# The first thirty products of a 392-product matmul stream: another order of loads, transposes and sums

## The chip, the cores and the metric

The kernel runs on one core of one Trainium2 chip. The metric is the time on the device in microseconds (us), the median of several executions. A core has five engines that run side by side, each through its own instructions in order: TensorE (PE, with weight loads listed apart as PEld), VectorE (DVE), ScalarE (ACT), GpSimd (POOL) and SyncE (SP), which here only issues DMAs. They wait for each other through semaphores.

## The reference

```python
x = L0_attn_data                       # (2, 1024, 512): 2048 rows of 512, float32
xn = _layernorm(x, axis=-1)            # (x - mean) / sqrt(var + 1e-5)
s = einsum('bsk,nk->bsn', xn, weight * block_mask)          # 512 x 512, mask by 32 x 32 blocks
nx = xn * rsqrt(mean(xn * xn) + 1e-5) * ln_w
h = silu(einsum('bsh,ih->bsi', nx, gate_w)) * einsum('bsh,ih->bsi', nx, up_w)   # 1792 columns
g = silu(einsum('bsi,hi->bsh', h, down_w))
x = x + s * g
```

## The kernel before

**Products.** All of it is float32. The wide products (gate and up together, and the masked linear) are done in two nested levels of Strassen's scheme in Winograd's form, which forms seven products in place of eight and pays for it with sums and differences. The rows of x are four tiles of 512 rows (t = 0 to 3); each tile is transposed on TensorE into four chunks of 128 features (c = 0 to 3), so that features lie on partitions. A product is a 128x128 weight times a 128x512 operand, two TensorE instructions of 0.43 us, 0.86 us in all. Seven products make one *instance* (function `instance`); there are 56 instances for the 7 gate and up groups and the masked linear, and a later stage of 7 more sets for the down projection. This text writes j:m for product m (1 to 7) of instance j. Only the start of this stream is changed: instances 0 to 3, which use tiles 0 and 1 alone.

**An instance.** Products 1, 6, 7 and 4 add up one after the other in one PSUM bank (call it x), 5 and 3 in a second (y), and 2 is added to the value that x had after product 1, in a third (z). Between two products of one bank the value has to be read out: the *snapshot* after 5 and after 6, the *total* after 2, 3, 7 and 4. Instances with an even number copy on ACT where nothing is to be added (`prior is None`), and those with an odd number add the even one's result on DVE. The value of x after product 1 gets into z by `seed`: an ACT copy into z's bank, to which product 2 is then added ("seeded", line 338); in instance 0 it goes into a buffer in SBUF instead and is added at the total.

**Operands.** `normalise` (L146 on DVE, L148 on ACT) applies the layer norm in place, from `stats` (L126, L127) and `factors` (L137 to L141, with a square root on ACT between two pieces on DVE). `transpose` (L155) writes a chunk into a PSUM bank, `evacuate` (L163) copies it to SBUF on ACT. `inner_b` forms the operands of products 5, 6, 7 and 4 as differences (all `add` calls have line L97); q 1 stands for instance 0 (chunks 0 and 1), q 2 for instance 1 (chunks 2 and 3). For 5, 6 and 7 one input comes straight from the bank of a transposed chunk of tile 1. So the bank of a chunk of tile 1 has two kinds of readers, ACT's copy and DVE's differences. `scale_a` multiplies the first weights by ln_w, `inner_a` forms sums of them on POOL.

**Banks.** PSUM has eight: three with tag X, two Y, one Z, two V (line 91). Transposed chunks share the tags of the products. A bank is handed on when all that read it are through.

**Order.** Nothing is scheduled by a planner. Every operation is put on a list with a position, `at(position, function)`, the list is sorted by position, and each engine runs its own operations in that order. A position is counted in products: 7j plus an offset for instance j. `T(us)` turns a wanted time into a position. `EARLY` gives single products another position than their instance would. `warm` has TensorE multiply the identity by itself until the first tile is there. Loads are issued at the very start, in the order in which they are called, nearly all by SP; each x tile is four loads of 256 KB, each first-level weight block is one of 256 KB.

The seven products of an instance, with offset, bank, snapshot and total, are this table:

```python
            (0, 1, "X", True, None, None),
            (2, 5, "Y", True, ("s5", 3), None),
            (3, 2, "Z", True, None, (None, 0)),
            (4, 6, "X", False, ("s2", 1), None),
            (6, 3, "Y", False, None, ("s2", 1)),
            (8, 7, "X", False, None, ("s5", 3)),
            (12, 4, "X", False, None, (None, 2)),
```

Of the kernel before, what the change touches and what calls it, by code (L numbers as in the profile page):

```python
# [14 lines left out]
P = 128  # L15
# [16 lines left out]
def tile_masked_linear_gated_ffn(  # L32
# [11 lines left out]
    nc = tc.nc  # L44
    NT, H = x.shape
    KC = H // P
    G = gu.shape[0]
    NTT = NT // W
    TT = W // P
# [16 lines left out]
    EARLY = {}  # L66

    def at(pos, fn, *args):
        events.append((pos, len(events), fn, args))
# [23 lines left out]
    def bank(tag, name):  # L93
        return ps.tile([P, W], F32, tag=tag, name=name, bufs=PSB[tag])

    def add(eng, o, a, b, op=ALU.add):
        eng.tensor_tensor(o, a, b, op)  # L97

    dve, pool, act = nc.vector, nc.gpsimd, nc.scalar


    lnw_sb = const.tile([P, KC], F32, tag="lnw", name="lnw_sb")
# [12 lines left out]
    agg = small.tile([P, NTT, TT, 2], F32, tag="agg", name="agg", bufs=1)  # L115
    rms = small.tile([P, NTT, TT], F32, tag="rms", name="rms", bufs=1)

    def load_x(t):
        for i in range(TT):
            xt[t, i] = mem[:, first_slot[("B6", "vc", "v5", "B4")[t]] + i, :]  # L120
            eng = nc.scalar if t == 0 and i >= 2 else nc.sync
            eng.dma_start(xt[t, i], x[(t * TT + i) * P : (t * TT + i + 1) * P, :])

    def stats(t, i):
        st = small.tile([P, 6], F32, tag="st", name=f"st_{t}_{i}")
# [42 lines left out]
    def rms_factor():  # L168

        def first():  # L170
            nc.vector.tensor_scalar_add(rms, agg[:, :, :, 1], EPS)
            nc.vector.reciprocal(rms, rms)
            nc.vector.tensor_mul(rms, agg[:, :, :, 1], rms)
            nc.vector.tensor_scalar_add(rms, rms, EPS)
        return [first, lambda: nc.scalar.activation(rms, rms, AF.Sqrt)]
# [136 lines left out]
    def inner_a(g, part, k0=0, n=2):  # L312

        if part == 1:
            i, si, qs = F["a1"] + 2 * (g % 3), F["s"] + 2 * (g % 2), (1, 2)
        else:
            i, si, qs = *w_slots(g), BLOCKS
        a, s = slots(i + k0, n), slots(si + k0, n)
        a11, a21, a12, a22 = (a[:, :, k * P : (k + 1) * P] for k in range(4))
        s1, s2, s3, s4 = (s[:, :, k * P : (k + 1) * P] for k in range(4))  # L320
        for k in range(n):
            aop[g, qs[k0 + k]] = {1: a11[:, k], 2: a12[:, k], 3: s4[:, k], 4: a22[:, k],
                                  5: s1[:, k], 6: s2[:, k], 7: s3[:, k]}
        return [lambda: add(pool, s1, a21, a22), lambda: add(pool, s2, s1, a11, ALU.subtract),
                lambda: add(pool, s4, a12, s2, ALU.subtract), lambda: add(pool, s3, a11, a21, ALU.subtract)]
# [7 lines left out]
    def instance(j, g, q, prior, dest, after):  # L333


        st = {}

        seeded = j > 0

        def mm(m, tag, key, first):  # L340
            if first and key not in st:
                st[key] = bank(tag, f"{key}_{j}")
            nc.tensor.matmul(st[key], weights(g, q, m), operand(q, m), start=first and not (key == "z" and seeded),  # L343
                             stop=True, skip_group_check=True)

        def seed():

            if seeded:
                st["z"] = bank("Z", f"z_{j}")
                nc.scalar.copy(st["z"], st["x"])  # L350
            else:
                st["s1"] = slot("s2", f"s1_{j}")
                nc.scalar.copy(st["s1"], st["x"])

        def snap(key, name, i):
            s = st[name] = slot(name, f"{name}_{j}")
            if prior is None:
                nc.scalar.copy(s, st[key])
            else:
                add(dve, s, st[key], prior(i))  # L360

        def total(key, name, i):
            if key == "z" and not seeded:
                name = "s1"
            if name:
                add(dve, dest(i), st[key], st[name])
            elif prior is None:
                nc.scalar.copy(dest(i), st[key])
            else:
                add(dve, dest(i), st[key], prior(i))  # L370

        at(EARLY.get((j, 0), 7 * j + 1), seed)
        for off, m, tag, first, snapshot, out in (
# [8 lines that stand above are left out]
            key, pos = tag.lower(), 7 * j + off  # L382
            at(EARLY.get((j, m), pos), mm, m, tag, key, first)
            if snapshot:
                at(pos + 1, snap, key, *snapshot)
            elif out:

                pos += 2.3 if prior is None and m == 2 and seeded else 1
                at(pos, total, key, *out)
                after(out[1], pos)  # L390

# [261 lines left out]
    where = {gq: j for j, gq in enumerate(order)}  # L653
    N = len(order)
    END = 7 * N
    T = lambda us: (us - 14.9) / 0.86
    EARLY.update({(0, 1): T(11.5), (0, 0): T(12.6), (1, 1): T(12.7), (0, 2): T(12.8)})
    SILU = 26.2
    at(T(-10), load_x, 0)
    at(T(-10), lambda: nc.sync.dma_start(lnw_sb, ln_w))  # L660
    for K in range(2):
        at(T(-10), load_a, 0, K)
    at(T(-10), load_x, 1)
    for K in range(2):
        at(T(-10), load_a, 1, K)
    at(T(-10), load_x, 2)
# [4 lines left out]
    def plan(pos, step, todo):  # L671
        for i, fn in enumerate(todo):
            at(pos + step * i, fn)


    def warm(n, b):
        for _ in range(n):
            nc.tensor.matmul(b[:, :P], ident, ident, start=True, stop=True, skip_group_check=True)

    at(T(1.4), lambda: warm(30, bank("V", "idle")))  # L680
    for t, p, step in ((0, T(8.2), 0), (1, T(13.4), 0), (2, 14.5, 1.3), (3, 22.0, 1.3)):
        plan(p, step, factors(t))
    for i in range(TT):
        half = act if i < 2 else dve
        at(T(4.5 + 0.85 * i), stats, 0, i)
        at(T(9.0 + 0.7 * (i % 2)), normalise, 0, i, half)
        at(T(10.1 + 0.8 * i), stats, 1, i)
        at(T(14.2 + 0.7 * (i % 2)), normalise, 1, i, half)
        for c in range(KC):
            at(T((10.2, 10.6, 11.0, 11.8)[c] + 0.1 * i), transpose, 0, c, (2, 3, 0, 1)[i], "XYYX"[c])  # L690
            at(T(15.3 + 0.4 * c + 0.1 * i), transpose, 1, c, (2, 3, 0, 1)[i], "XVVY"[c])
    at(T(6.0), scale_a, 0, 0, pool)
    at(T(8.2), scale_a, 0, 1, pool)
    for c in range(KC):
        at(T((10.7, 11.3, 11.9, 14.0)[c]), evacuate, 0, c, act)
        at((5.6, T(16.0), 6.0, 3.14)[c], evacuate, 1, c, act)
    for us, q, m in ((15.9, 1, 5), (16.6, 1, 6), (17.2, 1, 7), (17.8, 2, 5), (18.4, 1, 4), (19.0, 2, 6),
                     (19.6, 2, 7), (20.3, 2, 4)):
        at(T(us), inner_b, q, m, dve)
    for q in (1, 2):  # L700
        for k in (0, 1):
            for n in (0, 1):
                at(8, outer_b, q, k, n, None)
    at(T(16.4), scale_a, 1, 0)
    at(5.2, scale_a, 1, 1)
    for i in range(TT):
        at(9.6 + 1.2 * i, stats, 2, i)
        at(17.2 + 1.3 * i, stats, 3, i)
        at((30.2, 37.0, 40.9, 44.0)[i], normalise, 2, i, act)
        at(26.5 + 2.4 * i, normalise, 3, i, dve)  # L710
    plan(22.2, 1.3, rms_factor())

    for t, p0 in ((3, 37.5), (2, 51.5)):
        n = t % 2
# [21 lines left out]
    for g in range(G + 1):  # L736
        p, rest = 7 * where[g, 1], 7 * where[g, BLOCKS[0]]
        for K in range(2):
            if g > 2:
                at(p - 22, load_a, g, K)  # L740
            if g == G:
                at(p - (10.4, 7.3)[K], lambda K=K: mask_a(aq[G, 0, K], 0, K))
            elif g > 1:
                at(p - (10.4, 7.3)[K], scale_a, g, K)
        if g:
            plan(p - 7, 1, inner_a(g, 1))
        else:
            plan(T(7.4), 0, inner_a(0, 1, 0, 1))
            plan(T(10.0), 0, inner_a(0, 1, 1, 1))
        at(rest - 29, load_block, g)  # L750

        def block_sums(g=g):
            for k, fn in enumerate(outer_a(g)):
                todo[g, k] = fn
        at(rest - 20, block_sums)
        if g == G:
            for k, (R, K) in ((1, (1, 0)), (4, (1, 1)), (0, (0, 0)), (3, (0, 1))):
                at(rest - 20.5, lambda k=k, R=R, K=K: mask_a(wblk[G][k], R, K))
        for k, off in enumerate((-19.9, -19.3, -18.1, -17, -15.95, -15.94, -15.93, -15.3, -13.95)):
            at(rest + off, lambda g=g, k=k: todo[g, k]())  # L760
        plan(rest - 13, 2.5, inner_a(g, 2, 0, 5))
# [131 lines left out]
```

## Time and profile before

| | |
|---|---|
| median of 4 runs | 520.54 us (519.5 to 520.89) |
| the profiled execution's own time | 519.5 us |
| its span | 517.7 us |
| TensorE busy | 507.8 us, 98% of the span |
| VectorE, GpSimd, ScalarE busy | 384.8, 342.2, 177.9 us |
| granted TensorE clock | full in every slice |

The span is counted from the first instruction to the last; 1.8 us of the execution's time lie around it. Views used: the timeline (start, duration, engine, line, operation, output and inputs, and in brackets the idle time of the engine before it and what ended it), the list of waits, stretches with the busy time of each engine, and DMA issues with their time to landing. TensorE's 98% include the warming up of the first 10 us. The prediction is about the stretch from 0 to 40 us, in which instances 0 to 3 and most of the preparation lie.

### The profile page before, as it was taken

The numbers are of one execution on the slowest core, as the hardware profiler recorded it, in microseconds if no ns is written. First come the engines' busy times: TensorE is split into PE (matmuls) and PEld (weight loads), VectorE is DVE, ScalarE is ACT, GpSimd is POOL, SyncE is SP. The second block draws the span as 40 slices with busy tenths as digits, with TensorE's granted clock in tenths as the row PEclk, the third lists the DMA queues.
The fourth block names the chain that finished last, engine by engine and source line by source line (L and its number), as shares of the span: only waits on it lengthen the run. The fifth ranks groups of instructions, "written<-read, shape, count | busy, mean of one in ns | idle before, by whom it ended". The sixth has DMA issues, their size and how long they took to land. (4 is left out here: it accounts for less than half of the span.)

```text
span 517.7 us, 4933 instructions
## 1 busy us (share of the span) xinstructions
PE 507.8 (98%) x1277; PEld 231.6 (45%) x1277; DVE 384.8 (74%) x583; ACT 177.9 (34%) x340; POOL 342.2 (66%) x280
## 2 busy tenths in 40 slices
PE   8999999999999999999999999998999999999997
PEld 8444543444444444444444444433444444444444
DVE  5897789876986969789696978979646654467726
ACT  3657644542536344353634434320100101001111
POOL 5422239852695978869597889979553664739960
PEclk9999999999999999999999999999999999999999
DMA  8435466459157574666988466598997599476372
GB/s 299 148 122 203 163 220 220 170 210 342 58 208 227 216 283 182 232 237 211 393 326 287 177 234 239 195 331 313 330 382 270 181 372 331 157 254 210 144 235 82
DMA packets 60460, 121.59 MB, mean 235 GB/s; under 512 B 5760, under 2 KB 13328, under 8 KB 58384
## 3 DMA queue, kind: packets, MB, share of 16 engines
q1 hardware_dynamic: 60144, 120.75, 65.1%
q10 hardware_dynamic: 288, 0.52, 0.3%
q8 instruction: 10, 0.16, 0.1%
q14 instruction: 18, 0.15, 0.1%
HBM read 75.11 MB, written 46.15 MB: 234 GB/s over the span
## 5 line engine op out<-in xcount | busy, mean ns | idle before, releaser
L97 POOL TENSOR_TENSOR mem<-mem 128x512 f32<-128x512 f32 (+4 forms) x243 | 306.3, 1283 | 139.8 <-ACT mem L264 45.6
L343 PE MATMUL x<-mem 128*128 128x512 f32 x448 | 214.3, 595 | 1.8 <-DVE mem L97 1.8
L343 PEld LDWEIGHTS x<-mem 128*128 128x128 f32 x448 | 83.4, 190 | 109.4 <-issue 85.0
L97 DVE TENSOR_TENSOR mem<-x,mem 128x512 f32<-128x512 f32 x136 | 91.8, 684 | 40.9 <-PE x L343 39.3
L343 PE MATMUL y<-mem 128*128 128x512 f32 x224 | 114.6, 593 | 1.6 <-DVE mem L97 1.5
L97 DVE TENSOR_TENSOR mem<-mem 128x512 f32<-128x512 f32 (+2 forms) x64 | 84.4, 1324 | 7.1 <-PE dx L570 4.4
L570 PE MATMUL dx<-mem 128*128 128x512 f32 x174 | 78.3, 592 | 0.0
L97 DVE TENSOR_TENSOR mem<-y,mem 128x512 f32<-128x512 f32 x96 | 65.6, 684 | 10.7 <-PE y L343 8.8
L343 PEld LDWEIGHTS y<-mem 128*128 128x128 f32 x224 | 42.1, 190 | 53.9 <-issue 46.3
L350 ACT COPY z<-x 128x512 f32<-128x512 f32 x55 | 31.5, 573 | 100.2 <-PE x L343 95.6
L343 PE MATMUL z<-mem 128*128 128x512 f32 x112 | 57.3, 593 | 0.5 <-ACT z L350 0.5
L570 PEld LDWEIGHTS dx<-mem 128*128 128x128 f32 x174 | 33.1, 190 | 41.6 <-issue 40.9
L570 PE MATMUL dy<-mem 128*128 128x512 f32 x98 | 44.5, 592 | 0.0
L404 ACT ACTIVATE gate<-mem 128x512 f32<-128x512 f32 x56 | 33.1, 601 | 27.7 <-DVE mem L97 23.3
L409 DVE TENSOR_TENSOR mem<-gate,mem 128x512 f32<-128x512 f32 x56 | 38.0, 681 | 4.5 <-POOL mem L97 3.7
L543 POOL TENSOR_TENSOR mem<-mem 128x512 f32<-128x512 f32 x16 | 25.4, 1596 | 15.8 <-DMA mem<-s_dram 15.6
L343 PEld LDWEIGHTS z<-mem 128*128 128x128 f32 x112 | 21.0, 190 | 26.7 <-issue 24.2
L97 DVE TENSOR_TENSOR mem<-z,mem 128x512 f32<-128x512 f32 x41 | 27.9, 682 | 4.4 <-PE z L343 3.0
L553 ACT ACTIVATE silu<-mem 128x512 f32<-128x512 f32 x15 | 9.0, 602 | 64.6 <-DVE mem L97 48.3
L570 PEld LDWEIGHTS dy<-mem 128*128 128x128 f32 x98 | 18.6, 190 | 23.4 <-issue 23.4
L97 DVE TENSOR_TENSOR mem<-dx,mem 128x512 f32<-128x512 f32 x16 | 11.0, 690 | 20.1 <-PE dx L570 20.1
L570 PE MATMUL dz<-mem 128*128 128x512 f32 x56 | 25.2, 592 | 0.0
(69 smaller groups left out, 280.5 us busy)
## 6 DMA issues: line engine op xcount, KB each, us to landing
h_dram<-mem SPq DMA_DIRECT2D x98, 256.0 KB, 2.1
mem<-h_dram SPq DMA_DIRECT2D x28, 768.0 KB, 6.3
mem<-in_gu SPq DMA_DIRECT2D x42, 256.0 KB, 4.2
acc_dram<-mem SPq DMA_DIRECT2D x8, 1024.0 KB, 3.9
mem<-acc_dram SPq DMA_DIRECT2D x8, 1024.0 KB, 4.8
s_dram<-mem SPq DMA_DIRECT2D x16, 256.0 KB, 2.4
mem<-s_dram SPq DMA_DIRECT2D x16, 256.0 KB, 6.5
mem<-in_x_t SPq DMA_DIRECT2D x16, 256.0 KB, 5.8
```

What stands on the lines that cost most here:

```text
L97: eng.tensor_tensor(o, a, b, op)
L343: nc.tensor.matmul(st[key], weights(g, q, m), operand(q, m), start=first and not (key == "z" and seeded), stop=True, skip_group_check=True)
L350: nc.scalar.copy(st["z"], st["x"])
L404: nc.scalar.activation(gate[key], t(), AF.Silu)
L409: nc.vector.tensor_mul(a(), gate[key], b())
L543: at_later.append(lambda: nc.gpsimd.tensor_tensor(s_tile, s_tile, rms_bc[t], ALU.mult))
L553: nc.scalar.activation(b[0][:, part], y[:, part] if source is None else source(), AF.Silu)
L570: nc.tensor.matmul(st[key], w(), b(), start=first and key != "z", stop=True, skip_group_check=True)
```

## The change

It touches positions and engines of the first 30 or so products and of what feeds them. Tile 0 is loaded by SP alone, its four loads in a row, where two of them were issued by ACT; ln_w's load goes from SP to ACT. The loads of tile 1 and of the first weights alternate. There are 25 warm-up products for 30. Product 1:2 comes fourth, before the transposes of tile 1; for that, instance 1 is no longer seeded: its z is a Y bank of its own, and DVE adds x and instance 0's result into a buffer, which the total adds to z. Two of the eight differences (the operands of 0:4 and 1:4, in the code `inner_b` with q 1 and 2, m 4) and the scaling of the second pair of weights go from DVE and ACT to POOL. Chunk 3 of tile 1 is transposed after the other chunks into a V bank, not a Y bank. Statistics of tile 2 come later by about four positions, and the positions of the rest are shifted.

```diff
@@ -115,11 +115,10 @@
     agg = small.tile([P, NTT, TT, 2], F32, tag="agg", name="agg", bufs=1)
     rms = small.tile([P, NTT, TT], F32, tag="rms", name="rms", bufs=1)
 
-    def load_x(t):
-        for i in range(TT):
+    def load_x(t, part=range(4)):
+        for i in part:
             xt[t, i] = mem[:, first_slot[("B6", "vc", "v5", "B4")[t]] + i, :]
-            eng = nc.scalar if t == 0 and i >= 2 else nc.sync
-            eng.dma_start(xt[t, i], x[(t * TT + i) * P : (t * TT + i + 1) * P, :])
+            nc.sync.dma_start(xt[t, i], x[(t * TT + i) * P : (t * TT + i + 1) * P, :])
 
     def stats(t, i):
         st = small.tile([P, 6], F32, tag="st", name=f"st_{t}_{i}")
@@ -335,11 +334,12 @@
 
         st = {}
 
-        seeded = j > 0
+        seeded = j > 1
+        zbank = "Y" if j == 1 else "Z"
 
         def mm(m, tag, key, first):
             if first and key not in st:
-                st[key] = bank(tag, f"{key}_{j}")
+                st[key] = bank(zbank if key == "z" else tag, f"{key}_{j}")
             nc.tensor.matmul(st[key], weights(g, q, m), operand(q, m), start=first and not (key == "z" and seeded),
                              stop=True, skip_group_check=True)
 
@@ -350,7 +350,10 @@
                 nc.scalar.copy(st["z"], st["x"])
             else:
                 st["s1"] = slot("s2", f"s1_{j}")
-                nc.scalar.copy(st["s1"], st["x"])
+                if prior is None:
+                    nc.scalar.copy(st["s1"], st["x"])
+                else:
+                    add(dve, st["s1"], st["x"], prior(0))
 
         def snap(key, name, i):
             s = st[name] = slot(name, f"{name}_{j}")
@@ -386,6 +389,8 @@
             elif out:
 
                 pos += 2.3 if prior is None and m == 2 and seeded else 1
+                if m == 2:
+                    pos = EARLY.get((j, "z"), pos)
                 at(pos, total, key, *out)
                 after(out[1], pos)
 
@@ -653,14 +658,16 @@
     where = {gq: j for j, gq in enumerate(order)}
     N = len(order)
     END = 7 * N
-    T = lambda us: (us - 14.9) / 0.86
-    EARLY.update({(0, 1): T(11.5), (0, 0): T(12.6), (1, 1): T(12.7), (0, 2): T(12.8)})
+    T = lambda us: (us - 14.4) / 0.86
+    EARLY.update({(0, 1): T(10.4), (1, 1): T(11.3), (0, 2): T(12.2), (1, 2): T(13.1), (0, 0): T(11.95),
+                  (1, 0): 4.5, (0, "z"): T(14.75), (1, "z"): 7.0})
     SILU = 26.2
     at(T(-10), load_x, 0)
-    at(T(-10), lambda: nc.sync.dma_start(lnw_sb, ln_w))
-    for K in range(2):
-        at(T(-10), load_a, 0, K)
-    at(T(-10), load_x, 1)
+    at(T(-10), lambda: nc.scalar.dma_start(lnw_sb, ln_w))
+    for part, K in (((0,), 0), ((1,), 1), ((2, 3), None)):
+        at(T(-10), load_x, 1, part)
+        if K is not None:
+            at(T(-10), load_a, 0, K)
     for K in range(2):
         at(T(-10), load_a, 1, K)
     at(T(-10), load_x, 2)
@@ -677,38 +684,38 @@
         for _ in range(n):
             nc.tensor.matmul(b[:, :P], ident, ident, start=True, stop=True, skip_group_check=True)
 
-    at(T(1.4), lambda: warm(30, bank("V", "idle")))
-    for t, p, step in ((0, T(8.2), 0), (1, T(13.4), 0), (2, 14.5, 1.3), (3, 22.0, 1.3)):
+    at(T(1.4), lambda: warm(25, bank("V", "idle")))
+    for t, p, step in ((0, T(6.9), 0), (1, T(12.55), 0), (2, 20.5, 1.3), (3, 22.6, 1.3)):
         plan(p, step, factors(t))
     for i in range(TT):
         half = act if i < 2 else dve
-        at(T(4.5 + 0.85 * i), stats, 0, i)
-        at(T(9.0 + 0.7 * (i % 2)), normalise, 0, i, half)
-        at(T(10.1 + 0.8 * i), stats, 1, i)
-        at(T(14.2 + 0.7 * (i % 2)), normalise, 1, i, half)
+        at(T(3.4 + 0.85 * i), stats, 0, i)
+        at(T(7.9 + 0.7 * (i % 2)), normalise, 0, i, half)
+        at(T(9.1 + 0.85 * i), stats, 1, i)
+        at(T(13.5 + 0.7 * (i % 2)), normalise, 1, i, half)
         for c in range(KC):
-            at(T((10.2, 10.6, 11.0, 11.8)[c] + 0.1 * i), transpose, 0, c, (2, 3, 0, 1)[i], "XYYX"[c])
-            at(T(15.3 + 0.4 * c + 0.1 * i), transpose, 1, c, (2, 3, 0, 1)[i], "XVVY"[c])
+            at(T((9.1, 9.9, 9.5, 10.3)[c] + 0.1 * i), transpose, 0, c, (2, 3, 0, 1)[i], "XYYX"[c])
+            at(T((14.7, 15.1, 15.5, 16.9)[c] + 0.1 * i), transpose, 1, c, (2, 3, 0, 1)[i], "XVVV"[c])
+    for c in range(KC):
+        at(T((9.7, 10.9, 10.3, 11.5)[c]), evacuate, 0, c, act)
+        at(T((19.2, 15.5, 19.8, 18.6)[c]), evacuate, 1, c, act)
+    for us, q, m, eng in ((15.3, 1, 5, dve), (15.9, 1, 6, dve), (16.6, 1, 7, dve), (17.2, 2, 5, dve), (17.8, 2, 6, dve),
+                          (18.4, 1, 4, pool), (19.9, 2, 7, dve), (19.7, 2, 4, pool)):
+        at(T(us), inner_b, q, m, eng)
     at(T(6.0), scale_a, 0, 0, pool)
-    at(T(8.2), scale_a, 0, 1, pool)
-    for c in range(KC):
-        at(T((10.7, 11.3, 11.9, 14.0)[c]), evacuate, 0, c, act)
-        at((5.6, T(16.0), 6.0, 3.14)[c], evacuate, 1, c, act)
-    for us, q, m in ((15.9, 1, 5), (16.6, 1, 6), (17.2, 1, 7), (17.8, 2, 5), (18.4, 1, 4), (19.0, 2, 6),
-                     (19.6, 2, 7), (20.3, 2, 4)):
-        at(T(us), inner_b, q, m, dve)
+    at(T(6.1), scale_a, 0, 1, pool)
+    for K in range(2):
+        at(T(14.3 + K), scale_a, 1, K, pool)
     for q in (1, 2):
         for k in (0, 1):
             for n in (0, 1):
                 at(8, outer_b, q, k, n, None)
-    at(T(16.4), scale_a, 1, 0)
-    at(5.2, scale_a, 1, 1)
     for i in range(TT):
-        at(9.6 + 1.2 * i, stats, 2, i)
-        at(17.2 + 1.3 * i, stats, 3, i)
+        at(13.5 + 1.2 * i, stats, 2, i)
+        at(18.4 + 1.2 * i, stats, 3, i)
         at((30.2, 37.0, 40.9, 44.0)[i], normalise, 2, i, act)
         at(26.5 + 2.4 * i, normalise, 3, i, dve)
-    plan(22.2, 1.3, rms_factor())
+    plan(23.0, 1.3, rms_factor())
 
     for t, p0 in ((3, 37.5), (2, 51.5)):
         n = t % 2
@@ -745,8 +752,8 @@
         if g:
             plan(p - 7, 1, inner_a(g, 1))
         else:
-            plan(T(7.4), 0, inner_a(0, 1, 0, 1))
-            plan(T(10.0), 0, inner_a(0, 1, 1, 1))
+            plan(T(10.5), 0, inner_a(0, 1, 0, 1))
+            plan(T(12.4), 0, inner_a(0, 1, 1, 1))
         at(rest - 29, load_block, g)
 
         def block_sums(g=g):
```

## The prediction

> **What bounds the kernel now.** I read the page first: TensorE is busy 98% of the span at the full clock, so what a change of the start is worth is how much sooner the stream of products runs without gaps. Then the timeline from 0 to 30 us, for these gaps.
>
> ```profile
> PE 507.8 (98%) x1277; PEld 231.6 (45%) x1277; DVE 384.8 (74%) x583; ACT 177.9 (34%) x340; POOL 342.2 (66%) x280
> ```
>
> ```profile
> 4.39 0.69 DVE L126 BATCH_NORM_STATS2 st<-mem 128x6 f32<-128x512 f32 x1 [4.39 <-DMA mem<-in_x]
> ...
> 8.88 1.52 ACT L148 ACTIVATE mem<-mem,nb,scl 128x512 f32<-128x512 f32 x2 [0.44 <-DVE nb L138]
> ...
> 11.23 1.56 ACT L163 COPY mem<-pt 128x512 f32<-128x512 f32 x3 [0.83 <-PE pt L155]
> ...
> 13.04 0.59 ACT L353 COPY mem<-x 128x512 f32<-128x512 f32 x1 [0.26 <-PE x L343]
> ...
> 14.34 1.52 ACT L148 ACTIVATE mem<-mem,nb,scl 128x512 f32<-128x512 f32 x2
> ...
> 16.71 0.59 ACT L163 COPY mem<-pt 128x512 f32<-128x512 f32 x1 [0.85 <-PE pt L155]
> ...
> 17.33 0.69 DVE L97 TENSOR_TENSOR mem<-pt,mem 128x512 f32<-128x512 f32 x1 [0.36 <-ACT mem L163]
> ...
> 19.97 1.10 PE L343 MATMUL x<-mem 128*128 128x512 f32 x2
> ...
> 21.16 1.10 PE L343 MATMUL y<-mem 128*128 128x512 f32 x2
> ...
> 21.64 0.59 ACT L163 COPY mem<-pt 128x512 f32<-128x512 f32 x1 [0.47 <-DVE mem L97]
> ...
> 22.77 1.12 PE L343 MATMUL z<-mem 128*128 128x512 f32 x2 [0.51 <-ACT z L350]
> ...
> 27.73 1.10 PE L343 MATMUL x<-mem 128*128 128x512 f32 x2 [0.41 <-DVE mem L97]
> ...
> 28.67 1.02 PE L343 MATMUL y<-mem 128*128 128x512 f32 x2
> ```
>
> See three things. 0:7 starts at 19.97, 2:5 at 28.67; between lie eight products of 0.86, 6.88 us, so 1.82 are lost: 1:5 waits for a bank, 1:2 (the z row) for ACT's seed, 1:7 for a snapshot queued on DVE between statistics. Second, two readers of one bank take turns in program order: DVE's difference at 17.33 waits for ACT's copy of that chunk (16.71 to 17.30), ACT's copy at 21.64 for DVE's difference. Third, from the timeline of 30 to 44 us:
>
> ```profile
> 35.40 0.41 DVE L173 TENSOR_TENSOR rms<-agg,rms 128x16 f32<-128x16 f32 x1
> ...
> 35.85 0.65 DVE L174 TENSOR_SCALAR rms<-rms 128x16 f32<-128x16 f32 x1
> ...
> 36.41 0.68 DVE L97 TENSOR_TENSOR mem<-x,mem 128x512 f32<-128x512 f32 x1
> ...
> 37.19 0.69 DVE L97 TENSOR_TENSOR mem<-y,mem 128x512 f32<-128x512 f32 x1
> ...
> 38.11 1.02 PE L343 MATMUL y<-mem 128*128 128x512 f32 x2
> ```
>
> The total of 2:7 (36.41) and the snapshot of 3:5 (37.19 to 37.88) end just before 2:4 (37.25) and 3:3 (38.11) need them. DVE is nearly without a pause from 17.3 to 44: a second bound, right beneath TensorE.
>
> **The change part by part.** *Loads.* Before, the first load shares the engines with ACT's and lands at 4.36 (3.6 after its issue). The stretches show 400 GB/s, 0.65 us for 256 KB, so alone it lands by 3.7; ln_w beside it costs about 0.1. I take 3.8; bounds 3.7 (nothing more, the warm-ups hide it) and 4.36 (0.4 later for all that follows). Two more SP issues at 0.43 each stay under the 0.65 of a transfer and cost nothing; past that, tile 0 would come late. Four statistics at 0.82 each, as in the rows, give normalising at 8.03 for 8.88. The first weights land one transfer later (7.75), POOL scales them until 9.6: hidden, 0:1 comes at 11.0.
>
> *Warm-ups.* Ten instructions fewer at 0.11 (20 in 2.0 us, less the overlap, in the stretch 6.5 to 8.5): the transposes start at 9.37 for 10.48. The last normalised piece is there at 8.03 + 1.52 = 9.55, chunk 0's last transpose at 9.70: the cover is 0.15.
>
> *Tile 1.* Chunk 0's copy starts at 10.12 (11.23 less 1.11); two of chunk 3's transposes stand ahead of 0:1 (11.0) and two behind it, until 12.33. On ACT chunk 3's copy (12.37) now stands before the seed (12.85) and the square root: 13.36, though DVE is ready at 12.6. Normalising follows 0.65 later as in the rows: 14.01 for 14.34. So of 1.1 us only 0.33 survive, because ACT is late next. Bounds: nothing gained, if DVE's two pieces are held longer beside POOL's sums (1.24 at 14.34, 1.14 for the first tile); 0.8 gained, if the square root goes as soon as DVE is ready. I take the middle, since ACT's order is fixed.
>
> *The fourth product.* 1:1 at 12.17, 0:2 at 13.03, 1:2 at 13.89 to 14.75: it ends as the first piece of tile 1 is ready, costs nothing there, and takes 0.86 and the 0.67 of the wait for its seed out of the later stretch. DVE pays one sum, 0.60 a piece back to back, for instance 1's buffer.
>
> *The chain after tile 1.* Shifted by 0.33: chunk 1's copy 16.38 to 16.97, and behind it DVE: 0:6's operand 17.00, then 17.61, 18.21 and 1:6's at 18.81 to 19.49. Chunk 3's bank is chunk 1's, free at 17.69; its last transpose starts at 18.07, so 0:6 at 18.18 for 18.25. Chunk 3's copy now stands behind 1:6's operand, and ACT keeps its order: copy 19.53, snapshot for 0:7 20.02 to 20.61, chunk 0 20.51, chunk 2 20.99 to 21.57. TensorE waits: 0:7 at 20.68 for 19.97. DVE waits too: 1:7's operand reads chunk 2's bank, 21.61 instead of 20.01, then total 0:3 22.21 to 22.89, total 1:2 22.81, total 0:7 23.41. 1:5 wants a Y bank: 22.96, when PE was free at 21.62. Then seven products, 1:5 to 2:5, without a wait (snapshots at 24.10 and 24.96, statistics behind them): 2:5 at 28.20 for 28.67, a gain of 0.47.
>
> *DVE behind it.* From the first difference to the total of 2:7 it does two sums fewer for POOL, the totals 0:2 and 1:2 are earlier, one sum more; but it stands idle longer: 1.60 before 1:7's operand, 0.39 before 0:6's, 0.9 in waits for products, in sum 2.9 for 1.0 before (0.45, 0.33 and 0.18, the starts in the rows less 0.60). Counted on by 0.60 a sum, 0.82 a statistic: snapshot 1:6 24.96, statistic 25.56, total 1:3 26.68 (waits for 1:3), statistics 27.28 and 28.09, total 1:7 28.91, three statistics, total 1:4 31.97, statistic 32.64, total 2:3 33.46, statistic 34.06, factors and rms rows 34.97, 1.64 long as before: the total of 2:7 starts at 36.61 for 36.41. 2:4 would start at 37.37 for 37.25, 3:3 at 38.31 for 38.11: 0.2 lost. The two long rms rows end with POOL sums (POOL's four last from 33.45 to 36.47); these come about 0.45 earlier, and the last row, without POOL beside it, takes 0.2: total at 36.2, and 2:4 and 3:3 come 0.25 to 0.3 early. Between +0.2 and -0.47, I take -0.2.
>
> *POOL.* Scaling 1.83 a pair, differences 1.3 to 1.4 each (POOL's 128x512 sums average 1.283): weights ready by 19.4, 0:4's operand by 20.8, needed at 24.76; instance 2's sums by 23 for 28.2. Covered by 4 us. The Trainium skill, "GPSIMD Engine Reference", section Key points, speaks against it: GpSimd shares its SBUF interfaces with VectorE, and instructions with two SBUF inputs contend. The rows: such a DVE sum takes 0.68 at 21.53 beside POOL and 0.68 at 19.73 without; only the small rms rows show it. By the rows the sum is as above; the rule gives no price, one is bounded below.
>
> *To the end.* Later waits (0.8 before the mask product, 2.8 between 347 and 361) hang on DVE and POOL, which are idle 44 to 66 us for PE and start again from it: the shift passes on. Statistics of tile 2 are wanted only by normalising at position 30: nothing. The profiled execution's 519.5 becomes 519.3, the median's 520.54 becomes **520.3**.
>
> **The rivals.** *A, the bank does not hold 1:7's operand* (faster): if chunk 2's copy is through earlier, or the two readers overlap, DVE goes on at 20.16, behind chunk 3's copy; 1:5 follows 0:7 at 21.6, 2:5 at 26.9, and DVE's count puts the total of 2:7 at 35.2, 1.2 earlier: 519.3. For it: ACT's work in between is only copies of 0.5. Against it: both rows of turns.
>
> *B, 1:2's own bank* (little): if 1:5 gets the bank of 1:2, it waits for total 1:2, 0.6 more. For it: both free at one position. Against it: in the rows 1:5 took the bank freed first. DVE's count gives +0.4: 520.9.
>
> *C, POOL slows DVE* (slower): POOL is now busy from 15.3 to 25, where it was idle until 20.78. If each DVE sum pays what normalising paid there (at the longest 0.68, in the first 16 us where POOL works; median 0.54), 0.14 more, the ten sums on the chain give 1.4, less 0.2: 521.7. It decides from 0.13 each. For it: 0.65 and 0.41 for rms rows. Against it: 0.68 twice.
>
> **How the numbers follow.** 0.2%, 1.04 us, is about what a measurement here can tell from no change. Forecast 0.38, its own range 520.0 to 521.0; A 0.34, B 0.13, C 0.15. Faster: 0.28 of A, 0.02 of the forecast. Slower: 0.12 of C, 0.04 of B, 0.02. Same: the rest, 0.52. The range reaches to A with 0.3 beyond it (part of its 0.34 lies lower, where the square root is early too) and nearly to C: 519.0 to 521.6, which leaves out some 0.1 below and 0.08 above.
>
> **What would show it.** Right: first normalising near 8.0, second near 14.0 behind ACT's seed; 1:2 before tile 1's transposes; chunk 3's copy ended by DVE, 1:7's operand by ACT; 2:5 near 28.2. Wrong: no DVE wait near 20 (A), 1:5 behind total 1:2 (B), DVE sums over 0.75 (C), or a stream ahead at 28 and level at 40, then DVE is the bound.

## The result, and the profile after

The kernel after takes 521.19 us in the median of 44 runs (519.65 to 523.38), the kernel before 520.48 in 65 runs beside it (519.5 to 521.65): a ratio of 1.0015, with an interval of 1.0009 to 1.0021. It is 0.7 us slower. That lies inside the range and inside the bound of 0.2%, but on the other side of the forecast, which was 0.2 us faster. The profiled execution of the kernel after took 521.94 us, its span 520.2.

The busy line of the page says as little as before: TensorE 98% of the span.

```profile
PE 508.0 (98%) x1267; PEld 230.7 (44%) x1267; DVE 384.5 (74%) x582; ACT 175.5 (34%) x335; POOL 347.6 (67%) x286
```

The timeline of the kernel after, from 0 to 28 us (start, duration, engine, line, operation, and in brackets the idle time before and what ended it):

```profile
3.81 0.69 DVE L125 BATCH_NORM_STATS2 st<-mem 128x6 f32<-128x512 f32 x1 [3.81 <-DMA mem<-in_x]
...
7.88 0.69 DVE L125 BATCH_NORM_STATS2 st<-mem 128x6 f32<-128x512 f32 x1 [1.56 <-DMA mem<-in_x]
...
9.89 1.52 ACT L147 ACTIVATE mem<-mem,nb,scl 128x512 f32<-128x512 f32 x2 [0.66 <-DVE nb L137]
...
14.48 0.59 ACT L354 COPY mem<-x 128x512 f32<-128x512 f32 x1
...
15.62 1.52 ACT L147 ACTIVATE mem<-mem,nb,scl 128x512 f32<-128x512 f32 x2 [0.44 <-DVE nb L137]
...
21.38 0.59 ACT L162 COPY mem<-pt 128x512 f32<-128x512 f32 x1 [1.21 <-DVE mem L97]
21.86 0.59 ACT L361 COPY mem<-x 128x512 f32<-128x512 f32 x1
22.34 1.09 ACT L162 COPY mem<-pt 128x512 f32<-128x512 f32 x2
...
22.55 1.10 PE L343 MATMUL x<-mem 128*128 128x512 f32 x2 [0.77 <-POOL mem L97]
23.47 0.69 DVE L97 TENSOR_TENSOR mem<-mem,pt 128x512 f32<-128x512 f32 x1 [1.52 <-ACT mem L162]
...
24.90 1.10 PE L343 MATMUL y<-mem 128*128 128x512 f32 x2 [1.25 <-POOL mem L97]
```

Three readings. First, tile 0's first load lands as forecast (its statistic starts at 3.81), but the fourth keeps DVE waiting for 1.56, and normalising starts at 9.89 where 8.03 was forecast. Second, from there on nearly everything comes as worked out, only about 1.9 later (tile 1's normalising 1.6): chunk 3's copy waits for DVE (1.21), the snapshot behind it ends at 22.45 and lets 0:7 go, 1:7's operand waits for chunk 2's copy (1.52), and 1:5 waits behind that. Third, the releaser named for the two products is POOL, but that is only the work that ended last before them by the profile. For 0:7 I take it to be ACT's snapshot, which ends 0.10 before it, for 1:5 DVE's total of 0:3 (24.07 to 24.75), 0.15 before it: the run `e3_difference_first` below keeps POOL's order and has no 1.25, and in the profile of `e11_sums_on_dve` DVE is named for 1:5.

What the order itself costs is seen best when the loads are taken out, by counting from the first normalising. The last rows of the table go as far as 3:7. In each of these two lines, first of the kernel after and then of the kernel before, four instructions are two products, 4:1 and, 0.86 later, 3:7:

```profile
40.67 1.88 PE L343 MATMUL x<-mem 128*128 128x512 f32 x4
```

```profile
38.97 1.88 PE L343 MATMUL x<-mem 128*128 128x512 f32 x4
```


| from the first normalising to | forecast | measured in the kernel after |
|---|---|---|
| normalising of tile 1 | 14.01 - 8.03 = 5.98 | 15.62 - 9.89 = 5.73 |
| chunk 3's copy | 11.50 | 11.49 |
| 0:7 | 12.65 | 12.66 |
| 1:7's operand | 13.58 | 13.58 |
| 1:5 | 14.93 | 15.01 |
| 2:5 | 20.17 | 20.24 |
| 3:7 | 31.60 (39.83 before, less 0.2, less 8.03) | 41.53 - 9.89 = 31.64 |
| 3:7 in the kernel before | | 39.83 - 8.88 = 30.95 |

So the new order costs 0.69 more after the first normalising than the old one. It was to pay for that by having tile 0 earlier by 0.85. The experiments ask whether it has it, what makes the 0.69, and what else stands in the median.

### The profile page after: what moved, and what is told of

It reads as the page before. It is cut to its first block, busy times and chain, and to the rows that moved or that the text cites. A ratio compares the mean times of both kernels' runs of the same rounds, so it can differ in the third digit from the quotient of the medians.

```text
span 520.2 us, 4916 instructions
## 1 busy us (share of the span) xinstructions
PE 508.0 (98%) x1267; PEld 230.7 (44%) x1267; DVE 384.5 (74%) x582; ACT 175.5 (34%) x335; POOL 347.6 (67%) x286
## 5 line engine op out<-in xcount | busy, mean ns | idle before, releaser
L97 DVE TENSOR_TENSOR mem<-mem 128x512 f32<-128x512 f32 (+3 forms) x62 | 83.0, 1344 | 7.9 <-PE dx L575 4.2
```

## The experiments

Each kernel is the kernel after with the edit shown, unless said otherwise. Labels are shortened to e1 to e12. "Ratio" is to the kernel before on the same chip, with its 95% interval. The kernel before had a median of 520.33 beside e1 to e4, of 520.68 beside e5 to e8, and of 520.92 beside e9 to e12.

### The loads: where do they land?

`e1_two_queues`, tile 0 as in the kernel before:

```diff
-            nc.sync.dma_start(xt[t, i], x[(t * TT + i) * P : (t * TT + i + 1) * P, :])
+            eng = nc.scalar if t == 0 and i >= 2 else nc.sync
+            eng.dma_start(xt[t, i], x[(t * TT + i) * P : (t * TT + i + 1) * P, :])
...
-    at(T(-10), lambda: nc.scalar.dma_start(lnw_sb, ln_w))
+    at(T(-10), lambda: nc.sync.dma_start(lnw_sb, ln_w))
```

> The changed kernel with tile 0's loads as before: its third and fourth load issued by ACT, ln_w by SP. Theory L: the changed kernel's time is the forecast's chain plus a hold of tile 0's fourth load, which stood fourth in SP's row of DMAs in the profiled execution (landed 7.86, the third 5.16). Then the hold is gone from tile 0 (first normalising at 8.9, fourth load landed near 5.8), and what stays is the forecast's chain without the earlier landing: the last normalised piece at 10.4, chunk 0's last transpose 0.75 later than forecast, so -0.2 + 0.75: 521.0, with a narrow spread. Theory S: the hold was chance and the order of work behind tile 0 costs 0.7 by itself: with landings 0.85 later than forecast it is 0.7 + 0.75, 522.0.

Measured: 521.98, ratio 1.0038 (1.0022 to 1.0053). The number is theory S's, not theory L's; what makes it is told below the table.

`e2_before_one_queue`, the other way round, is the kernel before with nothing of the change but the row of loads on SP and ln_w on ACT:

```diff
-            eng = nc.scalar if t == 0 and i >= 2 else nc.sync
-            eng.dma_start(xt[t, i], x[(t * TT + i) * P : (t * TT + i + 1) * P, :])
+            nc.sync.dma_start(xt[t, i], x[(t * TT + i) * P : (t * TT + i + 1) * P, :])
...
-    at(T(-10), lambda: nc.sync.dma_start(lnw_sb, ln_w))
+    at(T(-10), lambda: nc.scalar.dma_start(lnw_sb, ln_w))
```

> The kernel before with one part of the change alone: tile 0's four loads by SP in a row, ln_w by ACT. Theory L: the fourth load is held in many executions; the 30 warm-ups hide a first normalising up to 9.3 (0.4 later than before), so a hold like the profiled one (normalising at 9.9) costs 0.6 and smaller ones nothing: 520.6 to 521.1, never faster, since the warm-ups end at 10.5. Theory S: landings are as forecast and hidden: 520.5, no change.

Measured: 520.48, ratio 0.9996 (0.9987 to 1.0004), no difference. Its profile has the normalising at 8.94, which the 30 warm-ups hide by theory L as well, so this run does not tell the two theories apart.

`e4_fourth_on_act` gives only the fourth load to ACT, behind ln_w:

```diff
+            eng = nc.scalar if t == 0 and i == 3 else nc.sync
...
-    at(T(-10), load_x, 0)
     at(T(-10), lambda: nc.scalar.dma_start(lnw_sb, ln_w))
+    at(T(-10), load_x, 0)
```

> The changed kernel with only tile 0's fourth load issued by ACT, behind ln_w; SP's fourth DMA is now tile 1's first load. Theory L with the place in SP's row as its cause: the hold moves to tile 1's first load, which is wanted only at 9.1; tile 0's loads land by 5.9, first normalising at 8.4 (first load 0.3 later beside ACT's), the stream 0.2 later than forecast: 520.5. If holds strike any load at random: 521.0 to 521.2, as the changed kernel. Theory S: 521.4.

Measured: 521.25, ratio 1.0025 (1.0014 to 1.0037), not the 520.5 of theory L.

`e8_lnw_on_sp` asks whether ACT's small ln_w load holds the row:

```diff
-    at(T(-10), lambda: nc.scalar.dma_start(lnw_sb, ln_w))
+    at(T(-10), lambda: nc.sync.dma_start(lnw_sb, ln_w))
```

> The changed kernel with ln_w's load back on SP, fifth, so that ACT issues no load at all. It tells what holds tile 0's loads. If a single row of DMAs cannot keep all transfers going at the start: the last landing again at 6.3 or later, first normalising at 8.4 or later, median 521.2. If ACT's small transfers (2 KB in pieces of 16 bytes) upset SP's row: last landing by 5.8, first normalising at 8.0, median 520.5.

Measured: 521.36, ratio 1.0016 (1.0004 to 1.0027). ACT issues no load at all there, and the third load still kept DVE waiting for 0.48.

`e12_alternate_rows` has both edits of e1, but with `i % 2` for `i >= 2`, so that SP and ACT take turns:

> The changed kernel with only tile 0's loads altered, in turn on SP and ACT, ln_w on SP. Theory L: last landing near 5.8, first normalising at 8.5, the stream 0.3 behind before, 520.8; theory G adds 1.5 in about one execution of four (both waits of TensorE are still there): median 521.0, highest above 522. If the hold is no matter of rows: last landing above 6.3, 521.2.

Measured: 522.3, ratio 1.0024 (1.0012 to 1.0035), where 521.0 was expected.

Every profile taken shows where tile 0 lands, so all of them speak on this:

| run | rows of tile 0 | last of four lands | first normalising | 3:7 | between |
|---|---|---|---|---|---|
| before | SP, ACT | 5.80 | 8.88 | 39.83 | 30.95 |
| e2 (before, one row) | SP | 6.65 | 8.94 | 40.01 | 31.07 |
| after | SP | 7.86 | 9.89 | 41.53 | 31.64 |
| e5 | SP | 7.09 | 9.12 | 40.75 | 31.62 |
| e7 | SP | 6.90 | 8.94 | 40.60 | 31.66 |
| e8 | SP | 6.38 | 8.48 | 41.76 | 33.27 |
| e11 | SP | 6.93 | 8.94 | 42.65 | 33.70 |
| e1 | SP, ACT | 5.98 | 9.02 | 40.73 | 31.71 |
| e4 | SP, ACT | 5.85 | 8.79 | 40.52 | 31.73 |
| e12 | SP, ACT | 5.68 | 8.65 | 40.40 | 31.74 |
| e3 | SP | 6.36 | 8.41 | 38.56 | 30.15 |
| e6 | SP | 5.93 | 8.04 | 39.06 | 31.02 |
| e9 | SP, ACT | 5.73 | 8.65 | 38.92 | 30.27 |
| e10 | SP | 6.97 | 8.98 | 39.16 | 30.17 |

With one row the last load lands anywhere from 5.93 to 7.86 and normalising starts at 8.94 in the median of nine profiles; with two rows it lands at 5.7 to 6.0, and normalising starts at 8.65 to 9.02. The first load is earlier in a row (3.79 for 4.36), and the last is not. In eight of the nine profiles with one row DVE stands still for the third or the fourth load, for 0.39 to 1.56 in all; e6 alone has no such wait. So 8.03 is the best case of a row (e6 had it, at 8.04), not the usual one, and the gain of 0.85 is usually nothing. That also is why e1, e4 and e12 are no better than the kernel after: two rows are steadier, but bring normalising forward by too little to pay 0.7 (in e4 DVE waits 0.67 for the second load). That the last column is 31.6 to 31.7 in after, e1, e4, e5, e7 and e12 shows that landing and order simply add up.

Theory L missed the medians of e1, e4 and e12 by 0.8 to 1.3. Its chain is in their profiles (31.71 to 31.74); three things were left out. Normalising came 0.15 to 0.4 later than it took for e4 and e12. From the last wide product to the end these three need 151.8 in place of 151.63, for a reason that stays open. And 10 of their 30 executions had a low clock (see below). By the profiles, normalising, chain and end put e1, e4 and e12 1.1, 0.9 and 0.75 behind the kernel before; their executions without the low clock are 1.2, 0.8 and 0.6 behind the kernel before beside them.

What the row loses is seen in the stretches of 1 us (busy time of PE, PEld, DVE, ACT and POOL, then clock, DMA share and GB/s), here of the kernel after

```profile
4.00:5.00 1.00, 1.00 (x7) 1.00 (x6) 0.97 (x3) 0.00 (x0) 0.00 (x0) 1.00 0.79 283
5.00:6.00 1.00, 1.00 (x7) 1.00 (x7) 0.96 (x3) 0.00 (x0) 0.00 (x0) 1.00 0.83 301
```

and of the kernel before:

```profile
4.00:5.00 1.00, 1.00 (x7) 1.00 (x6) 0.61 (x1) 0.00 (x0) 0.00 (x0) 1.00 1.05 406
5.00:6.00 1.00, 1.00 (x7) 1.00 (x7) 0.77 (x3) 0.00 (x0) 0.00 (x0) 1.00 1.08 367
```

283 and 301 GB/s against 406 and 367 are about 0.19 MB less in two microseconds, three quarters of one load of 256 KB. From 4 to 5 us all nine profiles with one row moved less (203 to 348 GB/s) than the five with two rows (377 to 410); from 5 to 6 us the two groups overlap (297 to 393, and 340 to 375). Why a row is held there, and at the third or fourth load, stays open; e8 excludes only the small load from ACT.

### The turns of two readers: what makes the 0.69?

`e3_difference_first` changes one position. Chunk 2's copy stands at T(19.8); 1:7's operand now reads that bank before it, not after:

```diff
-                          (18.4, 1, 4, pool), (19.9, 2, 7, dve), (19.7, 2, 4, pool)):
+                          (18.4, 1, 4, pool), (19.75, 2, 7, dve), (19.7, 2, 4, pool)):
```

> The changed kernel with one position altered: the difference for 1:7 (position 19.75 in place of 19.9) stands before ACT's copy of chunk 2, whose bank it reads, so it no longer waits for that copy. By the forecast's rival A it starts about 1.4 earlier, 1:5 does as well, and the stream gains 1.0 to 1.2 against the changed kernel: 520.1. Theory S, if its cost lies in this wait: the same gain. If VectorE were short of time for another reason (sums slowed beside GpSimd): under 0.4 gained, 520.9 or more.

Measured: 519.13, ratio 0.9983 (0.9973 to 0.9993), a larger gain than expected. From its timeline between 17 and 28 us:

```profile
19.89 0.59 ACT L162 COPY mem<-pt 128x512 f32<-128x512 f32 x1 [1.21 <-DVE mem L97]
...
20.50 0.69 DVE L97 TENSOR_TENSOR mem<-mem,pt 128x512 f32<-128x512 f32 x1
20.84 1.09 ACT L162 COPY mem<-pt 128x512 f32<-128x512 f32 x2
21.06 1.10 PE L343 MATMUL x<-mem 128*128 128x512 f32 x2 [0.76 <-POOL mem L97]
21.11 0.68 DVE L97 TENSOR_TENSOR mem<-y,mem 128x512 f32<-128x512 f32 x1
...
21.99 1.04 PE L343 MATMUL y<-mem 128*128 128x512 f32 x2
```

1:7's operand follows the copy of chunk 3 without the 1.52, and 1:5 starts 0.93 behind 0:7, not 2.35. Normalising to 3:7 takes 30.15 for 31.64: 1.49 less, with the same loads and the same work on POOL. This is the mechanism of rival A, which the change did not have by itself. So that one turn, 1:7's operand behind a copy that itself stands behind another turn, costs more than twice the 0.69 by which the new order is the longer one.

### The time of TensorE's waits: a second cost

The profile of e8 showed something that the kernel after had not: its 3:7 comes 33.27 behind the normalising, 1.64 more than the others. Up to 1:5 its distances are those of the kernel after (15.00); then come these stretches, a column each for PE, PEld, DVE, ACT and POOL, then the granted clock:

```profile
19.99:23.40 3.41, 1.47 (x3) 0.30 (x2) 1.89 (x4) 2.02 (x4) 3.33 (x4) 1.00 0.00 0
23.40:26.81 3.41, 3.33 (x4) 1.52 (x5) 1.82 (x3) 0.00 (x0) 1.43 (x3) 0.50 0.00 0
```

Right behind the waits ahead of 0:7 and 1:5 the clock is halved for 3.41 us, in which 4 matmuls begin where 8 would. The profile of e11 (below) has it too:

```profile
20.66:24.07 3.41, 1.28 (x3) 0.30 (x2) 3.41 (x5) 1.83 (x4) 3.01 (x4) 1.00 0.00 0
24.07:27.48 3.41, 2.89 (x4) 1.37 (x5) 2.26 (x4) 0.00 (x0) 0.00 (x0) 0.50 0.00 0
```

In both, the clock's first change of the execution lies 17.07 earlier, five times 3.41: the clock changes only on a grid of 3.41 us, which lies differently in each execution. (In the twelve other profiles the first change and the next are 512.0 or 515.41 apart, 150 or 151 times 3.413, and the first lies anywhere from 4.19 to 7.21.) By that grid the stretches just ahead of 24 us in two executions without a half clock are these, of e12

```profile
20.03:23.44 3.41, 1.72 (x4) 0.30 (x2) 1.89 (x4) 2.05 (x4) 2.92 (x4) 1.00 0.00 0
23.44:26.86 3.42, 3.09 (x8) 1.44 (x9) 3.17 (x6) 0.24 (x1) 1.17 (x2) 1.00 0.00 0
```

and of the kernel after:

```profile
20.86:24.28 3.42, 2.02 (x5) 0.39 (x3) 1.90 (x4) 2.05 (x4) 3.34 (x5) 1.00 0.00 0
```

TensorE busy for 1.28 or 1.47 of 3.41 us (38 and 43%) is followed by the half clock, for 1.72 or 2.02 (50 and 59%) it is not. At the end of e1's stream a stretch with 1.58 (46%, from 513.63) is not followed by it either. The two waits, 0.77 and 1.25, lie 3.12 from end to end, so whether one stretch holds enough of both depends on how the grid happens to lie. An estimate from these rows: with a threshold between 1.69 and 1.94 idle, 13 to 28% of the positions of the grid should lose a stretch; with e1's row, which sets it between 1.83 and 1.94, 13 to 20%. A lost stretch takes 0.0033 from the mean granted clock of an execution, so that it is seen in the runs without a profile too. With both waits left unfilled (after, e1, e4, e7, e8, e12, and e11, where the second is longer) 28 of 104 executions have a mean of 0.997 or less, 13 of 45 in the kernel after; with one wait or none (e3, e5, e6, e9, e10) 1 of 47; of the kernel before none of 85. In the kernel after the 13 have a median of 522.37, the other 32 of 520.94. The 28 are 27%, somewhat more than the narrower estimate. That e7 has none in 11 fits poorly with 27% (a chance of 3%). The rival theory that TensorE's idle time ahead of the transposes lowers the clock had forecast just that for e7, with its 30 warm-ups; but e3, e5, e6, e9 and e10 have the 25 warm-ups of the kernel after and 1 low execution in 47, so that idle time alone does not do it. Whether it has a part beside the two waits stays open.

The Trainium skill, "TensorE: Matmul & The Clock Gate", Part 1, section "What's actually happening", has a free-running window of 3413 ns, and throttles after an idle one. The length and the free running agree with the 3.41 and the 17.07 here; that the window must be idle doesn't, since 43% busy was too little.

Fillers that multiply the identity by itself, and whose product nobody reads, test it. `e5_filled`:

```diff
+    at(7.5, lambda: warm(3, bank("Z", "idle_1")))
+    at(8.5, lambda: warm(6, bank("Z", "idle_2")))
```

> The changed kernel with TensorE's two waits near 21 to 25 us (0.9 ahead of 0:7, 1.4 ahead of 1:5 in its profile) filled by 3 and 6 more multiplications of the identity into the free Z bank, which nothing reads. Theory G: 13 of 45 executions of the changed kernel show a mean granted clock of 0.997 or less and most of these take 1.5 longer; the clock is halved for some 3 us because of these two waits. Then no execution has it: median 520.8, the highest below 522.2. Theory L alone (landings make the whole loss, the clock has no part): no change of the share, median 521.2. If the early idle time of TensorE, before tile 0's transposes, is the cause of the lower clock, the share stays at 3 in 11.

Measured: 521.39, ratio 1.0006 (0.9995 to 1.0017). None of 12 executions had the low clock, as theory G forecast (a chance of 2% at 27%), and 1:5 still comes 15.00 behind the normalising: the fillers cost nothing there. The median is not the 520.8 of that theory: it gained little, if anything; 12 executions that scatter by 2 us do not show 0.25, which is what the 13 low ones add to the kernel after's median.

`e6_first_and_filled`, e3 with a filler between 0:7 and 1:5:

```diff
+    at(8.5, lambda: warm(4, bank("Z", "idle_2")))
...
-                          (18.4, 1, 4, pool), (19.9, 2, 7, dve), (19.7, 2, 4, pool)):
+                          (18.4, 1, 4, pool), (19.75, 2, 7, dve), (19.7, 2, 4, pool)):
```

> The altered position of the difference for 1:7 (which gave 519.13) with 4 multiplications of the identity in the one wait that is left there, 0.9 ahead of 1:5. Theory G: no execution under 0.998, median 519.0, the highest below 520.7. Theory L alone: 519.1 as before. If the fillers come in the way of 1:5: 519.3.

Measured: 520.52, ratio 0.9992 (0.9981 to 1.0003), worse than e3 in the median, with intervals that overlap. The filler stood where e3 has no wait any more, and pushed 1:5 to 14.47 behind the normalising, where e3 has 13.58. My expectation had overlooked that.

`e7_warm_30` puts the five warm-ups back:

```diff
-    at(T(1.4), lambda: warm(25, bank("V", "idle")))
+    at(T(1.4), lambda: warm(30, bank("V", "idle")))
```

> The changed kernel with 30 warm-ups, as before, in place of 25. They end 1.1 later, at 10.5. Where tile 0's loads are held (three profiles with one row of loads: last landing at 6.4, 6.7, 7.9 instead of 5.75) most of that is hidden. Theory L: the first transposes 0.2 to 1.1 later than in the changed kernel, by the size of the hold: median 521.5. Theory that the early idle time lowers the clock: that share vanishes, which gives back 0.4 on average: 521.1, the highest below 522.5. Theory G: the share stays at 3 in 11.

Measured: 521.48, ratio 1.001 (1.0001 to 1.0018). In its profile the warm-ups end at 10.49 and the transposes follow them without a wait, yet the first product comes 2.91 behind the normalising, where the kernel after has 2.82: with tile 0 as late as it is there, five warm-ups cost 0.09.

### The two sums on POOL: were they worth it?

`e11_sums_on_dve`:

```diff
-                          (18.4, 1, 4, pool), (19.9, 2, 7, dve), (19.7, 2, 4, pool)):
+                          (18.4, 1, 4, dve), (19.9, 2, 7, dve), (19.7, 2, 4, dve)):
```

> The changed kernel with the two moved differences (operands of 0:4 and 1:4) back on VectorE at their positions. They fall into VectorE's wait of 1.5 ahead of the difference for 1:7. If that wait hides them and GpSimd's sums neither helped nor harmed: 521.2, as the changed kernel, 1:5 at the same distance from the first normalising (15.0). If GpSimd's sums beside it slowed VectorE (rival C): 520.0 to 520.7. If moving them was a gain: 521.8 to 522.4.

Measured: 523.09, ratio 1.0036 (1.002 to 1.0052). Had they been hidden in DVE's wait of 1.52, the time would have stayed at 521.2. They aren't: 1:5 comes 15.65 behind the normalising for 15.01, and 3 of 7 executions have the low clock (the other four have a median of 521.91). The timeline of e11 from 20.8 to 23.3 us shows why:

```profile
20.84 2.99 POOL L97 TENSOR_TENSOR mem<-mem 128x256 f32<-128x256 f32 x3
20.92 2.33 DVE L97 TENSOR_TENSOR mem<-mem 128x512 f32<-128x512 f32 x2
...
23.17 0.67 DVE L97 TENSOR_TENSOR mem<-mem,pt 128x512 f32<-128x512 f32 x1
```

Two sums that took 0.68 each in the kernel before, one of them beside POOL, take 1.19 and 1.21 here (the last section shows the first apart). In the kernel after 1:7's operand starts 2.21 behind the sum before it, here 2.85: of the 2.25 for which the two sums hold DVE, 1.61 fall into the wait, and 0.64 remain. So moving them to POOL was a gain, and not a small one beside 0.7.

### Versions that beat both

`e10_first_filled_ahead` is e3 with the filler in the one wait that is left, ahead of 0:7:

```diff
+    at(7.5, lambda: warm(3, bank("Z", "idle_1")))
...
-                          (18.4, 1, 4, pool), (19.9, 2, 7, dve), (19.7, 2, 4, pool)):
+                          (18.4, 1, 4, pool), (19.75, 2, 7, dve), (19.7, 2, 4, pool)):
```

> As the run beside it, but with tile 0's loads in one row on SP as in the changed kernel. Theory L: first normalising anywhere from 8.0 to 9.9, the stream 0 to 1.6 ahead of before; median 519.6, wider spread than beside it. Theory G: no execution with a mean granted clock under 0.998.

Measured: 519.2, ratio 0.9969 (0.9957 to 0.998). `e9_first_alternate_filled` has these edits and those of e12:

> Three edits on the changed kernel: the difference for 1:7 ahead of chunk 2's copy, tile 0's loads in turn on SP and ACT (ln_w on SP behind them), and 3 multiplications of the identity in the wait ahead of 0:7 (position 7.5; the trial with 4 had them behind 0:7, where there is no wait, and they delayed 1:5 by 0.9). Theory L (one row of loads is held, two are not; hold and chain add up): landings near 4.4, 4.5, 5.5, 5.8, first normalising 8.5, stream 1.1 ahead of before: 519.3, highest below 520.7. If the order of the two rows makes no difference: as the trial with one row, 519.1 with single executions above 520.5.

Measured: 519.74, ratio 0.9973 (0.9963 to 0.9983). Both beat both kernels, as e3 does; one row or two makes no difference that these runs show. From the timeline of e10:

```profile
20.72 0.83 PE L685 MATMUL idle<-ident 128*128 128x128 f32 x6
...
21.65 1.10 PE L343 MATMUL x<-mem 128*128 128x512 f32 x2
...
22.59 1.04 PE L343 MATMUL y<-mem 128*128 128x512 f32 x2
```

TensorE is without a named wait from there to 2:5.

## Why the prediction was right and wrong

**The step that failed is *Loads*, in a term that it put at nothing: the waits for the third and the fourth load.** It let four statistics of 0.82 each follow the first landing at 3.8 without a pause, which gave normalising at 8.03. The first load came as forecast (3.44 to 3.81 in the nine profiles with one row), but in eight of the nine DVE then waited for the third or fourth, 0.39 to 1.56 in all, and 0.70 in the median of the nine, and normalising began at 8.04 to 9.89, 8.94 in the median. The sentence "past that, tile 0 would come late" named the risk, but looked for it in SP's issue, and the bounds given (3.7 and 4.36) were for the first load only; those behind it, which set normalising, had none. With 8.94 for 8.03 the working gives 0.9 more than 520.3, 521.2; the measured median is 521.19. So close an agreement is partly luck, since the median holds about 0.25 of low clock that was in no step. Why the row is held stays open.

**Warm-ups.** The cover of 0.15 was used up by the late landing: in the kernel after the transposes waited for DVE (at 10.63 and 11.24), not for the warm-ups. e7 shows how little hangs on them there.

**Tile 1, the fourth product and the chain after tile 1 were right.** Counted from the normalising, 0:7, 1:7's operand, 1:5 and 2:5 came within 0.08 of the forecast, with the releasers that it named for chunk 3's copy and for 1:7's operand. Tile 1's normalising was 0.25 better than the middle taken, inside the bounds, with its square root behind ACT's copy of 14.48 as forecast.

**DVE behind it was right, on its favourable side.** The total of 2:7 came 28.20 behind the normalising, where the two cases gave 28.17 and 28.58. Behind it 3:7 came at 31.64 for 31.60. The forecast gain of 0.2 was the sum of a gain in the loads (0.85) and a loss in the chain (0.65). The loss came (0.69); only the gain was missing.

**POOL was covered, but a row was misread.** Nothing on the chain waited for POOL's sums. The argument for it was the DVE sum at 21.53 of the kernel before, 0.68 beside POOL. That sum had begun first, and it was POOL that waited (the last section). Had the chain's sums had both operands in SBUF, rival C would have been the case, and at 0.5 for a sum that comes second (1.19 for 0.68), not at the 0.14 put down for it.

**The rivals.** A is not what the change does, but e3 shows its mechanism and price: 1.49, where 1.0 lay between A's 519.3 and the forecast. B fell: 1:5 followed the total of 0:3, as forecast. C fell: the chain's sums took 0.68 to 0.69, which fits the last section, since each of them has one operand in PSUM. **What none of them named** is the half clock, though the two waits that go with it were both in the text.

**The last step, "the shift passes on", holds exactly at first and then only roughly.** From 3:7, the 28th of the wide products, to the 271st all fourteen profiles need 214.56 to 214.65. The stretch from the 271st to the 291st took 17.47 in the profile of the kernel before and 17.69 to 19.25 in the others, whatever their start, by waits of TensorE for ACT and DVE ahead of the 275th, 277th and 287th; the stretch from there to the 392nd varies too, from 93.8 to 94.9. The profiled execution of the kernel before was its fastest of 65. Why these stretches vary stays open; it is as large as what was to be measured, so the two profiles differ by 2.5 in their span where the medians differ by 0.7.

## What to carry to other kernels

Bound the landing of every piece that a step needs, not of the first alone: here the first came 0.57 earlier and the last no earlier, and the order of the work was to be paid for with the first. Where two engines read one bank in turns, ask which of the readers has work queued behind it, and let that one read first; one position was worth 1.49 us here. And add up TensorE's waits over a few microseconds: two that cost 2.0 together went with another 1.4 in every fourth execution.

## What the runs showed of the hardware

**A DVE sum and a POOL sum exclude each other when both read SBUF alone.** The single instructions of the kernel before, first POOL's and then DVE's:

```profile
21.59 1.21 POOL L97 TENSOR_TENSOR mem<-mem 128x256 f32<-128x256 f32 x1
```

```profile
21.53 0.68 DVE L97 TENSOR_TENSOR mem<-mem 128x512 f32<-128x512 f32 x1
```

and of e11:

```profile
20.84 0.73 POOL L97 TENSOR_TENSOR mem<-mem 128x256 f32<-128x256 f32 x1
```

```profile
20.92 1.19 DVE L97 TENSOR_TENSOR mem<-mem 128x512 f32<-128x512 f32 x1
```

In e11 POOL began first: its sum ended at 21.57, 0.65 into DVE's, and DVE's then needed 0.54. In the kernel before DVE began 0.06 earlier, kept its 0.68, and POOL's sum took 1.21 in place of 0.73. The same holds later in the kernel before: of its DVE sums of this shape with both operands in SBUF, the one at 99.43 began when a POOL sum had 1.16 to go, and took 1.71. With one operand in PSUM nothing is seen: 242 such sums of the kernel after that began while a POOL sum was running took 0.67 to 0.69.

The Trainium skill, "SBUF — State Buffer", section "SBUF: two separate sides", says this: the pair of ports that DVE and GpSimd share is an exclusive lock, the one that starts first holds it for its whole instruction, and an operation of DVE takes part when it has two inputs in SBUF. The rows above agree.

**TensorE's clock** was halved after a stretch of 3.41 us with 38 or 43% busy, and not after one with 46, 50 or 59%, as told above.

**A single row of loads** at the very start moved 203 to 348 GB/s from 4 to 5 us (nine profiles), where two rows moved 377 to 410 (five profiles); the row's fourth load landed from 5.93 to 7.86, the last load of two rows from 5.68 to 5.98.
